# Gate products by Strassen's algorithm in a float32 graph network kernel

## The chip, the cores and the metric

One core of a Trainium2 chip. The metric is the device time of one execution in microseconds; medians of several runs are quoted. The engines are TensorE (PE; its weight loads are shown as PEld), VectorE (DVE), ScalarE (ACT), GpSimd (POOL) and the DMA queues. TensorE writes its products to PSUM, which these programs divide into eight banks; another engine then copies them to SBUF, the memory that holds all other tiles, and this copy is called an eviction. The granted clock is the share of its full clock that TensorE was given. Executions of one kernel agree within some 0.3%.

## The reference, cut to what matters

Sixty-four graphs of 256 nodes with 256 features go through three steps of a gated graph network (a GRU cell on aggregated messages), a residual and a layer norm, then through one graph attention layer with another residual and norm. All is float32.

```python
def _gru_cell(inp, h, w_ih, w_hh, b_ih, b_hh):
    gi = inp @ w_ih.T + b_ih              # 256 -> 768
    gh = h @ w_hh.T + b_hh                # 256 -> 768
    i_r, i_z, i_n = jnp.split(gi, 3, axis=-1)
    h_r, h_z, h_n = jnp.split(gh, 3, axis=-1)
    r = jax.nn.sigmoid(i_r + h_r)
    z = jax.nn.sigmoid(i_z + h_z)
    n = jnp.tanh(i_n + r * h_n)
    return (1.0 - z) * n + z * h

for i in range(L):                        # L = 3
    m = jnp.einsum('bnd,de->bne', h, weight[i])
    aggr = jnp.einsum('bst,bsd->btd', A, m)
    h = _gru_cell(aggr, h, w_ih, w_hh, b_ih, b_hh)
# then residual + layer norm, graph attention, residual + layer norm
```

## The kernel before

Graphs go through in pairs. A tile of [feature, (graph, node)] has 2 x 512 columns on 128 partitions and is the moving operand of the gate products, so each product has 512 columns. `weight[i] @ w_ih.T` is formed once. Two pairs are under way, half a pair apart; each yields between its steps, and the steps alternate, so that TensorE works on one pair while the other engines finish a step of the other. A scheduler then fixes the order of instructions on each engine. What follows the last n product of a layer until the new state is there (tanh, subtraction, product, sum) is called the tail.

```python
ps_t = ctx.enter_context(tc.tile_pool(name="ps_t", bufs=4, space=PSUM))   # transposes, small products
ps_g = ctx.enter_context(tc.tile_pool(name="ps_g", bufs=4, space=PSUM))   # gate products

def gates(i, e, ag, hT, hT_new, name):            # e: half of the 256 outputs
    def product(o, parts):
        pt = ps_g.tile([P, GN], F32, tag="g", name=f"pg_{name}_{o}")
        todo = [(w, m, d) for w, m in parts for d in range(C)]
        for n, (w, m, d) in enumerate(todo):
            nc.tensor.matmul(pt, w[:, d, o * P:(o + 1) * P], m[:, d, :],
                             start=(n == 0), stop=(n == len(todo) - 1))
        return pt
    hid, inp = (whhT, hT), (wc[:, i], ag)
    hn = product(2 * C + e, [hid])
    r_p = product(e, [hid, inp])
    ...                                            # sigmoid, n = tanh((hn + b) * r + n_p + b)
    nc.gpsimd.tensor_sub(d, hT[:, e, :], n)
    nc.vector.tensor_mul(d, d, z)
    nc.vector.tensor_add(hT_new[:, e, :], d, n)

steps = 3 + 3 * L + 2
while started < NP or active:
    if started < NP and (not active or (len(active) == 1 and active[0][1] >= steps // 2)):
        active.append([pair(started), 0])
        started += 1
    for a in list(active):
        ...                                        # one step of each pair
```

## Time and profile before

| | before |
|---|---|
| time, median | 2844.3 us |
| TensorE busy | 2803.1 us, 99% |
| TensorE's waits, summed | 30 us |
| VectorE / ScalarE / GpSimd busy | 1185.5 / 776.6 / 358.0 us |
| granted TensorE clock | 0.996 |

The page's first lines give the busy time of each engine and its share of the span, and the number of instructions. In a line of groups, the part ahead of the first bar names source line, engine, operation and tiles; then come busy time and the mean of one instruction; then the time the engine stood idle just before them and what ended it.

### The profile page before, as it was taken

How to read it: one execution, taken by the hardware profiler on the slowest of the kernel's cores; microseconds unless marked ns; L12 is line 12 of the kernel's file. 1: busy time of each engine (PE TensorE's matmuls, PEld its weight loads, DVE VectorE, ACT ScalarE, POOL GpSimd, SP SyncE). 2: the span in 40 equal slices, each digit the busy share in tenths (PEclk: the TensorE clock that was granted, in tenths of full speed). 3: DMA queues.
4: the chain of work that ended last, by engine and by line, in shares of the span. 5: the costliest groups of instructions: out<-in, count | busy, mean ns of one | idle time of the engine just before them, and what ended most of it. 6: DMA issues, size and time to landing. Idle time of an engine off the chain costs nothing.

```text
span 2842.6 us, 23364 instructions
## 1 busy us (share of the span) xinstructions
PE 2803.1 (99%) x8928; PEld 1560.3 (55%) x8928; DVE 1185.5 (42%) x2387; ACT 776.6 (27%) x1357; POOL 358.0 (13%) x362
## 2 busy tenths in 40 slices
PE   7999999999999999999999999999999999999996
PEld 4555555555555555555555555555555555555554
DVE  2344444444443444434443444443444444434434
ACT  1223222222322223222323222222222222222231
POOL 1111111111111111111111111111111111111111
PEclk9999999999999999999999999999999999999998
DMA  3000000000000000000000000000000000000000
GB/s 89 8 15 23 15 23 15 15 23 22 15 16 22 15 22 15 23 15 17 21 23 15 23 15 15 23 19 19 15 23 15 23 15 23 15 15 15 8 0 15
DMA packets 53518, 54.44 MB, mean 19 GB/s; under 512 B 1696, under 2 KB 53408, under 8 KB 53408
## 3 DMA queue, kind: packets, MB, share of 16 engines
q1 hardware_dynamic: 52256, 51.91, 5.6%
q8 instruction: 70, 1.15, 0.2%
q10 hardware_dynamic: 1056, 1.05, 0.1%
q14 instruction: 40, 0.33, 0.0%
q0 software_dynamic: 96, 0.01, 0.0%
HBM read 36.18 MB, written 16.78 MB: 19 GB/s over the span
## 4 chain that ended last, share of the span: by engine, by line
PE 98%; DVE 1%; DMA 0%; ACT 0%; issue 0%; POOL 0%; SPq 0%; POOLq 0%; DVEq 0%; ACTq 0%
PE pg L191 69%; PE pa L181 12%; PE pwh L270 4%; PE po L303 4%; PE pt L171 3%; PE s L263 2%; PE pt L162 2%; PE pt L294 1%; PE pw L138 1%; DMA adj<-in_adj_dram 0%; DVE d L210 0%; ACT z L207 0%; DVE hT L211 0%; PE pw L126 0%; DVE v L307 0%
## 5 line engine op out<-in xcount | busy, mean ns | idle before, releaser
L191 PE MATMUL pg<-ag,wc 128*128 128x512 f32 x2304 | 1051.4, 592 | 0.0
L191 PEld LDWEIGHTS pg<-ag,wc 128*128 128x128 f32 x2304 | 437.8, 190 | 551.0 <-issue 551.0
L191 PE MATMUL pg<-hT,whhT 128*128 128x512 f32 x1536 | 712.0, 592 | 0.0
L191 PEld LDWEIGHTS pg<-hT,whhT 128*128 128x128 f32 x1536 | 281.9, 190 | 278.8 <-issue 275.0
L202 DVE SCALAR_TENSOR_TENSOR n<-pg,bh,r 128x512 f32<-128x512 f32 x192 | 143.9, 750 | 603.8 <-ACT r L199 603.8
L199 ACT ACTIVATE r<-pg,b_sum 128x512 f32<-128x512 f32 x192 | 131.9, 687 | 859.8 <-PE pg L191 859.4
L191 PE MATMUL pg<-xT,whhT 128*128 128x512 f32 x768 | 350.5, 592 | 0.0
L210 DVE TENSOR_TENSOR d<-d,z 128x512 f32<-128x512 f32 x192 | 132.6, 691 | 522.0 <-ACT z L207 450.0
L209 POOL TENSOR_TENSOR d<-hT,n 128x512 f32<-128x512 f32 x128 | 162.1, 1267 | 1041.4 <-ACT n L204 1041.4
L181 PE MATMUL pa<-A,h 128*128 128x256 f32 x1024 | 239.3, 382 | 0.0
L204 ACT ACTIVATE n<-n,bi 128x512 f32<-128x512 f32 x192 | 138.5, 722 | 349.2 <-DVE n L203 349.2
L191 PEld LDWEIGHTS pg<-xT,whhT 128*128 128x128 f32 x768 | 143.5, 190 | 155.2 <-issue 146.1
L207 ACT ACTIVATE z<-pg,b_sum 128x512 f32<-128x512 f32 x192 | 132.1, 688 | 322.0 <-PE pg L191 322.0
L181 PEld LDWEIGHTS pa<-A,h 128*128 128x128 f32 x1024 | 191.9, 190 | 51.1 <-DVE h L72 12.1
L209 POOL TENSOR_TENSOR d<-xT,n 128x512 f32<-128x512 f32 x64 | 81.0, 1266 | 563.0 <-ACT n L204 563.0
L203 DVE TENSOR_TENSOR n<-n,pg 128x512 f32<-128x512 f32 x192 | 132.2, 689 | 32.5 <-PE pg L191 26.0
L211 DVE TENSOR_TENSOR hT<-d,n 128x512 f32<-128x512 f32 x192 | 131.9, 687 | 3.4
L171 PEld LDWEIGHTS pt<-ident,hT 128*128 128x128 f32 x768 | 88.4, 141 | 52.6 <-DVE hT L211 31.6
L270 PE MATMUL pwh<-gw,yT 128*128 128x257 f32 x512 | 116.7, 380 | 0.0
L303 PE MATMUL po<-wh,eT 128*128 128x256 f32 x512 | 116.5, 381 | 0.0
L181 PE MATMUL pa<-A,x 128*128 128x256 f32 x512 | 115.7, 379 | 0.0
L270 PEld LDWEIGHTS pwh<-gw,yT 128*128 128x128 f32 x512 | 97.5, 190 | 28.3 <-issue 8.5
(84 smaller groups left out, 1860.4 us busy)
## 6 DMA issues: line engine op xcount, KB each, us to landing
x<-in_x_dram SPq DMA_DIRECT2D x32, 512.0 KB, 3.8
adj<-in_adj_dram SPq DMA_DIRECT2D x32, 512.0 KB, 3.9
out_dram<-o SPq DMA_DIRECT2D x32, 512.0 KB, 2.9
wi_n<-in_L_gnn_w_ih_dram SPq DMA_DIRECT2D x1, 768.0 KB, 6.6
w_n<-in_L_gnn_weight_dram ACTq DMA_DIRECT2D x1, 768.0 KB, 9.4
wh_n<-in_L_gnn_w_hh_dram SPq DMA_DIRECT2D x1, 768.0 KB, 11.1
gw<-in_L_gnn_W_dram ACTq DMA_DIRECT2D x1, 256.0 KB, 10.4
bi<-in_L_gnn_b_ih_dram POOLq DMA_DIRECT2D x1, 3.0 KB, 8.1
```

The lines of the kernel that those rows point to most:

```text
L171: nc.tensor.transpose(pt[:, (c * C + d) * P:(c * C + d + 1) * P], hT[:, d, (g * C + c) * P:(g * C + c + 1) * P], ident)
L181: nc.tensor.matmul(pt[:, g * N:(g + 1) * N], h[:, g, s, d * P:(d + 1) * P], A[:, g, s, :], start=(s == 0), stop=(s == C - 1))
L191: nc.tensor.matmul(pt, w[:, d, o * P:(o + 1) * P], m[:, d, :], start=(n == 0), stop=(n == len(todo) - 1))
L199: nc.scalar.activation(r, r_p, AF.Sigmoid, bias=b_sum[:, e:e + 1])
L202: nc.vector.scalar_tensor_tensor(n, hn, bh[:, 2 * C + e:2 * C + e + 1], r, op0=ALU.add, op1=ALU.mult)
L203: nc.vector.tensor_add(n, n, n_p)
L204: nc.scalar.activation(n, n, AF.Tanh, bias=bi[:, 2 * C + e:2 * C + e + 1])
L207: nc.scalar.activation(z, z_p, AF.Sigmoid, bias=b_sum[:, C + e:C + e + 1])
L209: nc.gpsimd.tensor_sub(d, hT[:, e, :], n)
L210: nc.vector.tensor_mul(d, d, z)
L270: nc.tensor.matmul(pt[:, :D + 1], yT[:, d, k * P:(k + 1) * P], gw[:, d, :], start=(d == 0), stop=(d == C - 1))
L303: nc.tensor.matmul(pt[:, c * D:(c + 1) * D], eT[:, g, j, c * P:(c + 1) * P], wh[:, g, j, :], start=(j == 0), stop=(j == C - 1))
```

## The change

The gate matrix for r and z is 512 x 256, for n 256 x 256, and the moving tile is 256 x 512. Each is cut in 2 x 2 blocks, and seven block products of 256 columns take the place of eight (Strassen's algorithm in the form with shared sums). The weights' block sums are formed once. The moving tile's four block sums are formed on GpSimd for the state (`hT`) and for the aggregate (`ag`), and the products are put together by five VectorE sums of 512 for r and z and five for n. The products share three PSUM banks for r/z and three for n, so two banks are left for all else. To fit in SBUF, several tiles lose their second buffer. The diff is cut to what matters, and its lines are drawn together in places.

```diff
-    ps_t = ... bufs=4     ps_g = ... bufs=4
+    ps_t = ... bufs=2     ps_g = ... bufs=6
+    def blocks(m, name):
+        t = work.tile([P, 4, N], F32, tag="t", name=f"t_{name}", bufs=4)
+        b11, b12, b21, b22 = m[:, 0, :N], m[:, 0, N:], m[:, 1, :N], m[:, 1, N:]
+        nc.gpsimd.tensor_sub(t[:, 0:2, :], m[:, :, N:], m[:, 0, :].rearrange("p (g n) -> p g n", g=G))
+        nc.gpsimd.tensor_add(t[:, 2, :], t[:, 1, :], b11)
+        nc.gpsimd.tensor_sub(t[:, 3, :], b21, t[:, 2, :])
+        return {1: b11, 2: b21, 3: b22, 4: t[:, 3, :], 5: t[:, 0, :], 6: t[:, 2, :], 7: t[:, 1, :]}
+    class Products:                       # three banks x[0..2]; s, u2, u3 in SBUF
+        def product(self, q):
+            bank, fresh = {1: (0, True), 2: (0, False), 6: (1, True), 7: (1, False), 4: (1, False),
+                           5: (2, True), 3: (2, False)}[q]
+            ...                           # 256-column matmuls into self.x[bank]
+            if q == 1:   self.load(self.s, x1)
+            elif q == 6: nc.vector.tensor_add(self.u2, self.s, x2)
+            elif q == 7: nc.vector.tensor_add(self.u3, self.s, x2); nc.vector.tensor_add(self.u3, self.u3, x3)
+            elif q == 3: nc.vector.tensor_add(self.u2, self.u2, x3)
+            elif q == 4: nc.vector.tensor_add(self.s, self.s, x2)
+    # in gates(), first half:
+        for q in (1, 6, 5):
+            rz.product(q)
+        nn.product(1)
+        rz.product(7); update(1, rz.c[3])
+        nn.product(6)
+        rz.product(2); reset(0, rz.c[0], b_sum)
+        nn.product(5)
+        yield
+    # second half:
+        rz.product(3); reset(1, rz.c[1], b_rz)
+        nn.product(7)
+        rz.product(4); update(0, rz.c[2])
+        nn.product(2); fresh(0, 0, nn.c[0]); fresh(1, 1, nn.c[3])
+        nn.product(3); fresh(0, 1, nn.c[1]); finish(0)
+        nn.product(4); fresh(1, 0, nn.c[2]); finish(1)
```

`reset`, `update` and `fresh` form r, z and the argument of n's tanh, in pieces of one graph. `finish` is the old tail: tanh on ScalarE, `h - n` on GpSimd, product and sum on VectorE.

More of the change, by code (lines that the diff above doesn't have):

```diff
@@ L57 @@
     io = ctx.enter_context(tc.tile_pool(name="io", bufs=3))
-    work = ctx.enter_context(tc.tile_pool(name="work", bufs=2))
-    ps_t = ctx.enter_context(tc.tile_pool(name="ps_t", bufs=4, space=bass.MemoryType.PSUM))
-    ps_g = ctx.enter_context(tc.tile_pool(name="ps_g", bufs=4, space=bass.MemoryType.PSUM))
+    ps_t = ctx.enter_context(tc.tile_pool(name="ps_t", bufs=2, space=bass.MemoryType.PSUM))
+    ps_g = ctx.enter_context(tc.tile_pool(name="ps_g", bufs=6, space=bass.MemoryType.PSUM))
     def bank(name):
@@ L87 @@
     nc.gpsimd.memset(half, -0.5)
-    wihT = const.tile([P, C, O], F32, name="wihT")
     whhT = const.tile([P, C, O], F32, name="whhT")
@@ L93 @@
     wa2 = const.tile([P, C, P], F32, name="wa2")
+    w_sums = const.tile([P, L + 1, 4, 3 * P], F32, name="w_sums")
     b_sum = const.tile([P, O // P], F32, name="b_sum")
+    b_rz = const.tile([P, C], F32, name="b_rz")
     bi = const.tile([P, O // P], F32, name="bi")
@@ L99 @@
     with tc.tile_pool(name="prep", bufs=1) as prep:
+        wihT = prep.tile([P, C, O], F32, name="wihT")
         wi_n = prep.tile([P, O // P, D], F32, name="wi_n")
@@ L111 @@
         nc.vector.tensor_add(b_sum, bi, bh)
+        nc.vector.tensor_sub(b_rz, b_sum[:, :C], b_sum[:, C:2 * C])
         for src, dst in ((wi_n, wihT), (wh_n, whhT)):
@@ L140 @@
                     evacuate(wc[:, i, d, o0:o1], pt[:, :o1 - o0])
+        for j, w in enumerate([whhT] + [wc[:, i] for i in range(L)]):
+            for (a0, a1), (b0, b1), (o0, o1) in (((0, D), (D, 2 * D), (0, D)),
+                                                 ((2 * D, 2 * D + P), (2 * D + P, O), (D, D + P))):
+                a11, a12, a21, a22 = w[:, 0, a0:a1], w[:, 1, a0:a1], w[:, 0, b0:b1], w[:, 1, b0:b1]
+                s1, s2, s3, s4 = (w_sums[:, j, k, o0:o1] for k in range(4))
+                nc.gpsimd.tensor_add(s1, a21, a22)
+                nc.vector.tensor_sub(s3, a11, a21)
+                nc.gpsimd.tensor_sub(s2, s1, a11)
+                nc.gpsimd.tensor_sub(s4, a12, s2)
         gwT = transposed(gw, "gwT")
@@ L151 @@
             nc.vector.tensor_copy(wa2[:, d, :], wa[:, 1:2].to_broadcast([P, P]))
+    work = ctx.enter_context(tc.tile_pool(name="work", bufs=2))
     def to_T(src, name):
@@ L184, in aggregate @@
         return ag
-    def gates(i, e, ag, hT, hT_new, name):
-        def product(o, parts):
-            pt = ps_g.tile([P, GN], F32, tag="g", name=f"pg_{name}_{o}")
-            todo = [(w, m, d) for w, m in parts for d in range(C)]
-            for n, (w, m, d) in enumerate(todo):
-                nc.tensor.matmul(pt, w[:, d, o * P:(o + 1) * P], m[:, d, :],
-                                 start=(n == 0), stop=(n == len(todo) - 1))
-            return pt
-        hid, inp = (whhT, hT), (wc[:, i], ag)
-        hn = product(2 * C + e, [hid])
-        r_p = product(e, [hid, inp])
-        r = work.tile([P, GN], F32, tag="r", name=f"r_{name}")
-        nc.scalar.activation(r, r_p, AF.Sigmoid, bias=b_sum[:, e:e + 1])
-        n_p = product(2 * C + e, [inp])
-        n = work.tile([P, GN], F32, tag="n", name=f"n_{name}")
-        nc.vector.scalar_tensor_tensor(n, hn, bh[:, 2 * C + e:2 * C + e + 1], r, op0=ALU.add, op1=ALU.mult)
-        nc.vector.tensor_add(n, n, n_p)
-        nc.scalar.activation(n, n, AF.Tanh, bias=bi[:, 2 * C + e:2 * C + e + 1])
-        z_p = product(C + e, [hid, inp])
-        z = work.tile([P, GN], F32, tag="z", name=f"z_{name}")
-        nc.scalar.activation(z, z_p, AF.Sigmoid, bias=b_sum[:, C + e:C + e + 1])
-        d = work.tile([P, GN], F32, tag="d", name=f"d_{name}")
-        nc.gpsimd.tensor_sub(d, hT[:, e, :], n)
-        nc.vector.tensor_mul(d, d, z)
-        nc.vector.tensor_add(hT_new[:, e, :], d, n)
@@ new lines, in rows, with __init__ @@
+    def rows(j, first, second, o0):
+        w = whhT if j == 0 else wc[:, j - 1]
+        n = first[1] - first[0]
+        s = [w_sums[:, j, k, o0:o0 + n] for k in range(4)]
+        return {1: w[:, 0, first[0]:first[1]], 2: w[:, 1, first[0]:first[1]], 3: s[3],
+                4: w[:, 1, second[0]:second[1]], 5: s[0], 6: s[1], 7: s[2]}
+    class Products:
+        def __init__(self, terms, tag, name, load):
+            self.terms, self.load = terms, load
+            self.x = [ps_g.tile([P, 2 * N], F32, tag="g", name=f"x{k}_{name}") for k in range(3)]
+            self.s, self.u2, self.u3 = (work.tile([P, 2 * N], F32, tag=f"{tag}{k}", name=f"{tag}{k}_{name}")
+                                        for k in ("s", "u", "v"))
+            self.c = [self.x[0], self.u2, self.s, self.u3]
+        def product(self, q):
+            bank, fresh = {1: (0, True), 2: (0, False), 6: (1, True), 7: (1, False), 4: (1, False),
+                           5: (2, True), 3: (2, False)}[q]
+            for half, parts in enumerate(self.terms):
+                for n, (w, m, e) in enumerate(parts):
+                    nc.tensor.matmul(self.x[bank][:, half * N:(half + 1) * N], w[q][:, e * P:(e + 1) * P], m[q],
+                                     start=(fresh and half == 0 and n == 0), stop=(n == len(parts) - 1),
+                                     skip_group_check=True)
+            x1, x2, x3 = self.x
+            if q == 1:
+                self.load(self.s, x1)
+            elif q == 6:
+                nc.vector.tensor_add(self.u2, self.s, x2)
+            elif q == 7:
+                nc.vector.tensor_add(self.u3, self.s, x2)
+                nc.vector.tensor_add(self.u3, self.u3, x3)
+            elif q == 3:
+                nc.vector.tensor_add(self.u2, self.u2, x3)
+            elif q == 4:
+                nc.vector.tensor_add(self.s, self.s, x2)
@@ new lines, in gates, with both, with_bias, reset @@
+    def gates(i, ag, hT, hT_blocks, hT_new, name):
+        ag_blocks = blocks(ag, f"ag_{name}")
+        def both(first, second, o0):
+            return (rows(0, first, second, o0), hT_blocks), (rows(i + 1, first, second, o0), ag_blocks)
+        def with_bias(dst, src):
+            for e in range(C):
+                nc.scalar.activation(dst[:, e * N:(e + 1) * N], src[:, e * N:(e + 1) * N], AF.Identity,
+                                     bias=b_sum[:, C + e:C + e + 1])
+        hid, inp = both((0, D), (D, 2 * D), 0)
+        rz = Products([[(*hid, e), (*inp, e)] for e in range(C)], "rz", f"rz_{name}", with_bias)
+        hid_n, inp_n = both((2 * D, 2 * D + P), (2 * D + P, O), D)
+        nn = Products([[(*hid_n, 0)], [(*inp_n, 0)]], "nn", f"nn_{name}", nc.scalar.copy)
+        r = work.tile([P, C, G, N], F32, tag="r", name=f"r_{name}")
+        z = work.tile([P, C, G, N], F32, tag="z", name=f"z_{name}")
+        n = work.tile([P, C, G, N], F32, tag="n", name=f"n_{name}")
+        d = r
+        def reset(g, src, bias):
+            for e in range(C):
+                nc.scalar.activation(r[:, e, g, :], src[:, e * N:(e + 1) * N], AF.Sigmoid, bias=bias[:, e:e + 1])
+        def update(g, src):
+            nc.scalar.activation(z[:, :, g, :], src.rearrange("p (e n) -> p e n", e=C), AF.Sigmoid)
+        def fresh(e, g, src):
+            nc.vector.scalar_tensor_tensor(n[:, e, g, :], src[:, :N], bh[:, 2 * C + e:2 * C + e + 1], r[:, e, g, :],
+                                           op0=ALU.add, op1=ALU.mult)
+            nc.vector.tensor_add(n[:, e, g, :], n[:, e, g, :], src[:, N:])
+        def finish(e):
+            n_e, d_e = (v[:, e].rearrange("p g n -> p (g n)") for v in (n, d))
+            nc.scalar.activation(n_e, n_e, AF.Tanh, bias=bi[:, 2 * C + e:2 * C + e + 1])
+            nc.gpsimd.tensor_sub(d_e, hT[:, e, :], n_e)
+            nc.vector.tensor_mul(d_e, d_e, z[:, e].rearrange("p g n -> p (g n)"))
+            nc.vector.tensor_add(hT_new[:, e, :], d_e, n_e)
+        for q in (1, 6, 5):
+            rz.product(q)
+        nn.product(1)
+        rz.product(7)
+        update(1, rz.c[3])
+        nn.product(6)
+        rz.product(2)
+        reset(0, rz.c[0], b_sum)
+        nn.product(5)
+        yield
+        rz.product(3)
+        reset(1, rz.c[1], b_rz)
+        nn.product(7)
+        rz.product(4)
+        update(0, rz.c[2])
+        nn.product(2)
+        fresh(0, 0, nn.c[0])
+        fresh(1, 1, nn.c[3])
+        nn.product(3)
+        fresh(0, 1, nn.c[1])
+        finish(0)
+        nn.product(4)
+        fresh(1, 0, nn.c[2])
+        finish(1)
@@ L237, in pair @@
         hT = to_T(x_sb, f"xT_{p}")
+        hT_blocks = blocks(hT, f"xT_{p}")
         yield
         h = x_sb
-        v = work.tile([P, G, C, D], F32, tag="v", name=f"v_{p}")
+        v = work.tile([P, G, C, D], F32, tag="v", name=f"v_{p}", bufs=1)
         for i in range(L):
@@ L243, in pair @@
             hT_new = work.tile([P, C, GN], F32, tag="hT", name=f"hT_{p}_{i}", bufs=4)
-            for e in range(C):
-                gates(i, e, ag, hT, hT_new, f"{p}_{i}_{e}")
-                yield
+            yield from gates(i, ag, hT, hT_blocks, hT_new, f"{p}_{i}")
+            yield
             hT = hT_new
             if i < L - 1:
+                hT_blocks = blocks(hT, f"hT_{p}_{i}")
                 h = work.tile([P, G, C, D], F32, tag="h", name=f"h_{p}_{i}")
@@ L263, in pair @@
             nc.tensor.matmul(s2, wa2[:, d, :], yT[:, d, :], start=(d == 0), stop=(d == C - 1))
-        wh = work.tile([P, G, C, D], F32, tag="wh", name=f"wh_{p}")
+        wh = work.tile([P, G, C, D], F32, tag="wh", name=f"wh_{p}", bufs=1)
         s1 = work.tile([P, K], F32, tag="s1", name=f"s1_{p}")
-        sc = work.tile([P, K, N], F32, tag="sc", name=f"sc_{p}")
+        sc = work.tile([P, K, N], F32, tag="sc", name=f"sc_{p}", bufs=1)
         for k in range(K):
@@ L276, in pair @@
         nc.vector.scalar_tensor_tensor(sc, sc, ALPHA, sc, op0=ALU.mult, op1=ALU.max)
-        em = work.tile([P, K, N], F32, tag="em", name=f"em_{p}")
+        em = work.tile([P, K, N], F32, tag="em", name=f"em_{p}", bufs=1)
         nc.gpsimd.memset(em, NEG_INF)
@@ L287, in pair @@
         yield
-        eT = work.tile([P, G, C, N], F32, tag="eT", name=f"eT_{p}")
+        eT = work.tile([P, G, C, N], F32, tag="eT", name=f"eT_{p}", bufs=1)
         for g in range(G):
@@ L308, in pair @@
                                                y[:, g, c, :], op0=ALU.mult, op1=ALU.add)
-        o_sb = work.tile([P, G, C, D], F32, tag="o", name=f"o_{p}")
+        o_sb = work.tile([P, G, C, D], F32, tag="h", name=f"o_{p}")
         layer_norm(v, o_sb, f"b_{p}")
```

## The prediction

> **What bounds the kernel now.** First I read the page's busy shares, its slices and the shares by engine of the chain that ended last, because they say which engine sets the time.
>
> ```profile
> PE 2803.1 (99%) x8928; PEld 1560.3 (55%) x8928; DVE 1185.5 (42%) x2387; ACT 776.6 (27%) x1357; POOL 358.0 (13%) x362
> ...
> PE 98%; DVE 1%; DMA 0%; ACT 0%; issue 0%; POOL 0%; SPq 0%; POOLq 0%; DVEq 0%; ACTq 0%
> ```
>
> TensorE (PE) is busy from end to end and makes up 98% of the chain. Everything else is hidden beside it. Next the groups, for the price of each operation:
>
> ```profile
> L191 PE MATMUL pg<-ag,wc 128*128 128x512 f32 x2304 | 1051.4, 592 | 0.0
> L191 PE MATMUL pg<-hT,whhT 128*128 128x512 f32 x1536 | 712.0, 592 | 0.0
> ...
> L202 DVE SCALAR_TENSOR_TENSOR n<-pg,bh,r 128x512 f32<-128x512 f32 x192 | 143.9, 750 | 603.8 <-ACT r L199 603.8
> ...
> L210 DVE TENSOR_TENSOR d<-d,z 128x512 f32<-128x512 f32 x192 | 132.6, 691 | 522.0 <-ACT z L207 450.0
> L209 POOL TENSOR_TENSOR d<-hT,n 128x512 f32<-128x512 f32 x128 | 162.1, 1267 | 1041.4 <-ACT n L204 1041.4
> ```
>
> The mean of one matmul (592 ns) contains overlap, so the rate is read from the timeline, where products follow each other without a gap:
>
> ```profile
> 1408.44 3.60 PE L191 MATMUL pg<-hT,whhT 128*128 128x512 f32 x8
> 1418.74 3.62 PE L181 MATMUL pa<-A,x 128*128 128x256 f32 x16
> 1418.74 3.21 PEld L181 LDWEIGHTS pa<-A,x 128*128 128x128 f32 x15 [0.24 <-issue]
> ```
>
> Eight of 512 columns start in 3.43 us (the next group starts at 1411.88), 0.43 us each; sixteen of 256 columns take the same, 0.215 us each. So 256 columns cost exactly half, although a weight load (0.19 us) then nearly fills its slot. A product in the program is two such instructions, so one 256-column product is 0.43 us. Groups of 24 gate instructions recur in the chain at 109.87 and 196.43 us: a pair of graphs takes 86.56 us, 32 pairs 2770, and 73 us are start and end.
>
> Last, the very end, where one pair runs alone and PE has to wait:
>
> ```profile
> 2810.82 1.94 PE L162 MATMUL pt<-ident,y 128*128 128x128 f32 x8 [4.62 <-DVE y L225]
> 2813.22 3.78 PE L263 MATMUL s<-yT,wa 128*128 128x512 f32 x4 [0.46 <-ACT yT L70]
> 2827.29 2.38 PE L294 MATMUL pt<-ident,sc 128*128 128x128 f32 x8 [6.57 <-ACT sc L284]
> ```
>
> The eight transposes take 1.04 us elsewhere and four 512-column instructions some 1.9. After gaps of 4.6 and 6.6 us they take twice that; the granted clock of the last 92 us is 0.88. A long PE gap costs more than itself.
>
> **What the Trainium skill says.** "TensorE: Matmul & The Clock Gate", Part 1, says that after an idle window of about 3.4 us the array runs at half clock until it has been busy for such a window. The three lines above agree. The same page, in its architectural detail, says that VectorE and ScalarE are strict first-in-first-out. The trace agrees in that every idle time there ends in one wait, and it means that an instruction waiting on GpSimd holds up all behind it. "GPSIMD Engine Reference", section 3.1, gives 4497 ns for a two-input add of 2048 elements. The trace has 1267 ns for 512; the line through both gives about 0.73 us for 256 (an estimate). "SBUF — State Buffer", Who interferes with whom, says that a VectorE instruction with two SBUF inputs and a GpSimd instruction that reads SBUF block each other for a whole instruction. In the stretch of the trace I looked at they never overlap, so no number is to be had before.
>
> **The change part by part.** Removed: the gates are 24 products of 512 columns per layer and pair, 24 x 0.86 = 20.6 us. Now they are 28 + 14 = 42 of 256, 42 x 0.43 = 18.1 us. Saved 2.5 us, times 96 layer-pairs = 247 us. With nothing else, 2844 becomes about 2600.
>
> Added on GpSimd: two sets of block sums per layer and pair, each 1.27 + 0.73 + 0.73 = 2.7 us, so 5.5 x 96 = 524 us more; 880 in all, no bound as a sum. Added on VectorE: ten sums of 512 (0.69 each) and the n gate in eight pieces of 256 (about 0.42 to 0.45) for four of 512; 6.9 + 3.4 + 2.8 = 13.1 us instead of 5.6. That is +7.5 x 96 = 720 us, 1900 in all, some 60 us of VectorE per pair, against about 79 us of PE. No engine becomes a bound by its sum. The question is latency.
>
> I therefore took the compiled order of the changed kernel on each engine for one pair in the steady state and laid these durations along it by hand, with 0.05 to 0.1 us per hand-over, 0.26 us from the last matmul to its reader, and about 0.60 us between independent VectorE sums of 512 (as before's timeline shows). PE work is 79.4 us per pair. The places where PE's next instruction isn't ready:
>
> 1. Layer 0, second half, **7.9 us**. PE has 16 gate products and 8 transposes, 7.9 us. VectorE has in that stretch the other pair's residual add and layer norm (until 5.3 us, with a wait for GpSimd's power in it), then twelve gate sums and n pieces up to 11.4. Then the tail: tanh 0.72, GpSimd subtraction 2 x 1.27, product and sum. The new state is there at about 15.8 us, and PE's next instruction transposes it.
> 2. Layer 1, first half, **3.2 us**. With two transpose banks for four, one of them held by the score row until the last score is read, each attention projection waits for the eviction of the one before (about 1.2). Then the aggregate's second half is evicted behind 3.7 us of masking on VectorE and needs 2.0 us of GpSimd before product 6 (1.7).
> 3. End of layer 1 into layer 2, **7.3 us**. The state is at 13.8, while PE is through with gates and attention output at 10.3 (3.5); the block sums of the state, 2.0 us on GpSimd, stand before the next hidden products (1.7); eviction behind the second layer norm (0.7); aggregate block sums (1.4).
> 4. Layer 2 into the next pair's layer 0, **1.7 us** for the aggregate's block sums. The state's transposes are hidden behind 11 us of gate products.
>
> Sum 20.1: a period of 79.4 + 20.1 = 99.5 us, times 32 = 3184. Start and end: 73 as before, about 10 for forming the weight sums on GpSimd, and I allow 30 more because a pair alone has nothing to fill these waits: **3297 us**. So the 8 us saved per pair come back as 20 us of waits.
>
> **The rivals.** (a) The waits are filled and the saving arrives: 2600 to 2750. For it: in before PE has almost no waits in the middle, and the changed order moves hidden products ahead of the aggregate as filler. Against it: that filler is already in my timetable, and in layer 0 nothing is left between the last gate product and the state. (b) Some of the waits are shorter than I lay them, saving and waits cancel, 2790 to 2900. This needs 12 of the 20 us to be wrong. (c) The waits have consequences. GpSimd's second subtraction blocks VectorE's product of two SBUF tiles (0.6 us at the end of layers 0 and 1, about 1.2 at the aggregate after layer 2: 2.4 per pair). The half clock after gap 1 costs about 2.5 us, as the last lines above show (1.9 + 3.8 us for what takes about 3), and sometimes 1 us after gap 3. Together up to 6 us per pair, 190 us: about 3480. (d) Weight loads become the bound at 256 columns: the 3.62 us line speaks against it.
>
> **Range and chances.** The timetable says 3297, (c) pulls up by as much as 190. My errors of a hand timetable (the same wait counted at two places, a reorder that hides one) and the author's evident care over the order of products pull down. I take **3280 us**, with 3040 to 3470 for 8 in 10: 12 to 25 us of waits and after-effects per pair. Slower by over 2%: 0.88; within 2%: 0.05; faster: 0.07.
>
> **What would show it.** PE's own work: gate matmuls of 256 columns, 8064 instructions, at 0.215 us, so PE busy near 2550 to 2650 in the longer span (about 80%). VectorE busy near 1900, GpSimd near 880. In the waits, the largest of PE should be the transposes waiting for the new state (VectorE's last sum), about 11 us per pair, then gate products waiting for GpSimd's block sums, about 5 to 6. The granted clock should be below 1 in the middle slices, which (c) needs. GpSimd or VectorE two-input instructions with longer durations than 1267 and 690 ns would show the port. I am wrong if PE stays above 95% busy, if VectorE's sums are shorter than 0.69 us, or if transposes of the state wait less than 3 us a pair.

## The result and the profile after

The changed kernel takes **3569.4 us**, against 2844.3: 1.255 times as long. It was predicted to be slower, 3280 us with a range of 3040 to 3470, so the direction came out, the waits nearly did, and the price of the half clock behind them did not: the measured time lies above the range.

The page of the changed kernel: busy shares, the granted clock in 40 slices, and the chain that ended last by engine.

```profile
PE 2864.1 (80%) x12384; PEld 2352.9 (66%) x12384; DVE 1962.8 (55%) x3740; ACT 906.9 (25%) x1837; POOL 938.1 (26%) x962
...
PEclk9999898989998998989999889989899898989898
...
PE 54%; DVE 26%; POOL 13%; issue 4%; ACT 3%; DMA 0%; POOLq 0%; DVEq 0%; ACTq 0%; SPq 0%
```

TensorE is busy for 80% of a longer span, and its busy time has grown by 61 us although it has an eighth less gate arithmetic. The clock is down in most slices (0.906 in the mean). The chain now runs through VectorE and GpSimd for 39% of the span.

The view of waits of the changed kernel, TensorE's own, with the total in us, the number and the longest:

```profile
PE pt L192 <- DVE hT L293: 357.8, 65, 7.3
PE x_rz L239 <- POOL t_ag L212: 215.7, 96, 3.9
PE x_rz L239 <- POOL t_hT L212: 38.5, 31, 1.5
PE x_nn L239 <- DVE nnv_nn L248: 25.0, 31, 0.8
PE pa L202 <- DVE wh L78: 20.9, 31, 0.7
```

All of TensorE's waits sum to 692 us, and 692 + 2864 = 3556 of the span of 3565. So there are two items to explain: waits of 662 us more than before, and 61 us more busy time where 247 less was expected.

The timeline of the changed kernel, TensorE in the stretch at the end of layer 0 and into layer 1 (start, duration, what, and idle time with its releaser):

```profile
1691.79 0.60 PE L183 MATMUL pt<-ident,y 128*128 128x128 f32 x4
1699.71 0.45 PE L192 MATMUL pt<-ident,hT 128*128 128x128 f32 x1 [7.33 <-DVE hT L293]
1699.95 1.06 PE L239 MATMUL x_rz<-hT,whhT 128*128 128x256 f32 x2
1700.81 1.70 PE L192 MATMUL pt<-ident,hT 128*128 128x128 f32 x7
1702.33 2.75 PE L371 MATMUL s<-yT,wa 128*128 128x512 f32 x4
```

A gap of 7.33 us, then half speed for some 4 us: a product of two 256-column instructions takes 1.06 us (0.59 elsewhere in the same view), and four of 512 columns, which reach into full speed again, 2.75 us. What VectorE did meanwhile, in the same stretch:

```profile
1694.36 0.42 DVE L286 TENSOR_TENSOR n<-n,nns_nn 128x256 f32<-128x256 f32 x1
1696.63 2.33 DVE L292 TENSOR_TENSOR r<-r,z 128x512 f32<-128x512 f32 x2 [1.86 <-POOL r L291]
1698.89 1.28 DVE L293 TENSOR_TENSOR hT<-r,n 128x512 f32<-128x512 f32 x2
```

VectorE ends the n pieces at 1694.78, 2.4 us after TensorE ran dry; then comes the tail through ScalarE and GpSimd, and the first of the two products (line 292) waits inside for GpSimd: the group of line 292 has a mean of 1379 ns where before's line 210 had 691 (in the changed kernel the median is 1733 and the least 677).

The other long gap, at the aggregate of layer 0, in TensorE's timeline:

```profile
1666.38 1.03 PE L239 MATMUL x_rz<-t_xT,w_sums 128*128 128x256 f32 x4
1671.02 1.22 PE L239 MATMUL x_rz<-t_ag,w_sums 128*128 128x256 f32 x2 [3.62 <-POOL t_ag L212]
1672.03 1.06 PE L239 MATMUL x_rz<-t_xT,w_sums 128*128 128x256 f32 x2
1672.88 1.91 PE L239 MATMUL x_rz<-t_ag,w_sums 128*128 128x256 f32 x4
```

VectorE and GpSimd ahead of it, from the same timeline:

```profile
1665.77 1.74 DVE L292 TENSOR_TENSOR r<-r,z 128x512 f32<-128x512 f32 x1 [2.23 <-POOL r L291]
1667.43 0.68 DVE L78 COPY ag<-pa 128x512 f32<-128x512 f32 x1
1668.19 1.64 POOL L211 TENSOR_TENSOR t_ag<-ag 128x512 f32<-128x512 f32 x1 [1.23 <-DVE ag L78]
1669.91 1.05 POOL L212 TENSOR_TENSOR t_ag<-t_ag,ag 128x256 f32<-128x256 f32 x1
```

The aggregate's products were through by 1664.81, but its eviction (line 78) stands behind the other pair's held-up product and comes at 1667.43; then the block sums take 1.64 and 1.05 us instead of 1.27 and 0.73.

How much the half clock costs can be read from the granted clock. These windows lie on the three stretches of half clock of one pair, behind the gap into layer 2 (3.54 us and soon 1.23 more), the gap of 3.62 and the gap of 7.33. After the length come the busy times of PE, PEld, VectorE, ScalarE and GpSimd with their instructions, then the clock:

```profile
1632.23:1639.06 6.83, 5.60 (x18) 4.22 (x17) 4.13 (x15) 0.59 (x1) 3.95 (x5) 0.50 0.01 2
1669.78:1676.60 6.82, 5.58 (x13) 4.51 (x14) 2.32 (x3) 0.00 (x0) 2.16 (x3) 0.50 0.00 0
1697.08:1703.91 6.83, 4.20 (x12) 2.97 (x13) 4.39 (x6) 0.59 (x1) 3.46 (x4) 0.50 0.01 2
```

Half of TensorE's busy time in them is lost: 2.8, 2.8 and 2.1 us, 7.7 us a pair. The clock record of the whole run has 97 such stretches; TensorE is busy for 492 us in them, so 246 us are lost. That is most of the 308 us (61 + 247) by which busy time is too long.

### The profile page after: what moved, and what is told of

Same layout as the page of the kernel before. It is cut to its first block, busy times and chain, and to the rows that moved or that the text cites. A ratio compares the mean times of both kernels' runs of the same rounds, so it can differ in the third digit from the quotient of the medians.

```text
span 3565.2 us, 32872 instructions
## 1 busy us (share of the span) xinstructions
PE 2864.1 (80%) x12384; PEld 2352.9 (66%) x12384; DVE 1962.8 (55%) x3740; ACT 906.9 (25%) x1837; POOL 938.1 (26%) x962
## 3 DMA queue, kind: packets, MB, share of 16 engines
q10 hardware_dynamic: 1056, 1.05, 0.1%
## 4 chain that ended last, share of the span: by engine, by line
PE 54%; DVE 26%; POOL 13%; issue 4%; ACT 3%; DMA 0%; POOLq 0%; DVEq 0%; ACTq 0%; SPq 0%
PE x_rz L239 27%; PE x_nn L239 10%; PE pa L202 5%; DVE r L292 5%; POOL t_ag L211 4%; PE pwh L378 4%; POOL r L291 3%; PE pt L192 3%; DVE n L284 3%; PE s L371 2%; POOL t_ag L212 2%; DVE n L286 2%; ACT n L290 2%; DVE ag L78 2%; DVE hT L293 1%
## 5 line engine op out<-in xcount | busy, mean ns | idle before, releaser
L239 PE MATMUL x_rz<-t_ag,w_sums 128*128 128x256 f32 x1152 | 393.6, 442 | 215.7 <-POOL t_ag L212 215.7
L192 PE MATMUL pt<-ident,hT 128*128 128x128 f32 x768 | 174.2, 370 | 357.8 <-DVE hT L293 357.8
L239 PEld LDWEIGHTS x_rz<-t_ag,w_sums 128*128 128x128 f32 x1152 | 243.4, 219 | 290.7 <-POOL t_ag L212 254.3
L291 POOL TENSOR_TENSOR r<-hT,n 128x512 f32<-128x512 f32 x128 | 159.7, 1270 | 724.1 <-ACT n L290 724.1
L292 DVE TENSOR_TENSOR r<-r,z 128x512 f32<-128x512 f32 x192 | 259.8, 1379 | 153.5 <-POOL r L291 153.5
L239 PE MATMUL x_rz<-t_hT,w_sums 128*128 128x256 f32 x768 | 257.2, 426 | 38.5 <-POOL t_hT L212 38.5
L202 PE MATMUL pa<-A,h 128*128 128x256 f32 x1024 | 242.3, 385 | 20.9 <-DVE wh L78 20.9
L239 PE MATMUL x_rz<-ag,wc 128*128 128x256 f32 x768 | 228.4, 379 | 0.0
L239 PEld LDWEIGHTS x_rz<-t_hT,w_sums 128*128 128x128 f32 x768 | 154.8, 211 | 67.7 <-POOL t_hT L212 50.9
L239 PE MATMUL x_rz<-hT,whhT 128*128 128x256 f32 x512 | 173.4, 423 | 0.0
L239 PE MATMUL x_nn<-t_ag,w_sums 128*128 128x256 f32 x576 | 171.3, 379 | 0.0
## 6 DMA issues: line engine op xcount, KB each, us to landing
wh_n<-in_L_gnn_w_hh_dram SPq DMA_DIRECT2D x1, 768.0 KB, 11.2
```

Source lines behind the costliest of these rows:

```text
L192: nc.tensor.transpose(pt[:, (c * C + d) * P:(c * C + d + 1) * P], hT[:, d, (g * C + c) * P:(g * C + c + 1) * P], ident)
L202: nc.tensor.matmul(pt[:, g * N:(g + 1) * N], h[:, g, s, d * P:(d + 1) * P], A[:, g, s, :], start=(s == 0), stop=(s == C - 1))
L239: nc.tensor.matmul(self.x[bank][:, half * N:(half + 1) * N], w[q][:, e * P:(e + 1) * P], m[q], start=(fresh and half == 0 and n == 0), sto ...
L291: nc.gpsimd.tensor_sub(d_e, hT[:, e, :], n_e)
L292: nc.vector.tensor_mul(d_e, d_e, z[:, e].rearrange("p g n -> p (g n)"))
```

## The experiments

Times are medians. "Waits" is the sum of TensorE's waits in the profile, "busy" its busy time; together they make up the span within 0.7%. Kernels named b_ start from the kernel before, e_ from the changed one; all e_ kernels give right results.

| run | us | ratio to before | waits | busy | clock |
|---|---|---|---|---|---|
| before | 2844 | 1 | 30 | 2803 | 0.996 |
| changed | 3569 | 1.255 | 692 | 2864 | 0.906 |
| b_21 (wrong result) | 2618 | 0.921 | 53 | 2556 | 0.995 |
| b_256 | 2852 | 1.003 | 31 | 2810 | 0.996 |
| b_ps26 | 2941 | 1.034 | 96 | 2831 | 0.996 |
| e_warm | 3521 | 1.238 | 430 | 3081 | 0.971 |
| e_warm2 | 3423 | 1.204 | 369 | 3043 | 0.988 |
| e_dvefin | 3354 | 1.179 | 572 | 2774 | 0.931 |
| e_order | 3355 | 1.180 | 597 | 2748 | 0.945 |
| e_stag4 | 3559 | 1.252 | 691 | 2859 | 0.898 |
| e_all | 3229 | 1.135 | 476 | 2742 | 0.931 |
| e_three0 | 3299 | 1.160 | 483 | 2804 | 0.947 |
| e_three | 2971 | 1.045 | 263 | 2692 | 0.978 |
| e_three2 | 2969 | 1.044 | 271 | 2687 | 0.976 |
| e_three5 | 2940 | 1.034 | 277 | 2648 | 0.989 |
| e_three3 | 2892 | 1.017 | 211 | 2666 | 0.980 |
| e_three4 | 2920 | 1.027 | 217 | 2693 | 0.975 |
| e_three6 | 2824 | 0.993 | 174 | 2632 | 0.991 |
| e_three7 | 2915 | 1.026 | 236 | 2670 | 0.985 |

### Is the saving real? b_21 and b_256

b_21 leaves 3 of the 24 products out of the kernel before and adds nothing, so it has Strassen's arithmetic without its price.

```diff
             todo = [(w, m, d) for w, m in parts for d in range(C)]
+            if o >= 2 * C and parts[0][1] is hT or o == 2 * C - 1:
+                todo = todo[:-1]
```

> The kernel before with 3 of the 24 gate products per layer and pair left out, so TensorE's arithmetic is that of Strassen and nothing is added; the result is wrong on purpose. Theory A (the saving in arithmetic is real, 2.58 us per layer and pair): 2590 to 2615 us with TensorE still above 97% busy. Theory B (the other engines could not keep up even then): above 2680.

2618.5 us, 3.5 above theory A's range, with TensorE 98% busy. Busy time fell by 246.8 us, the predicted 247 almost to the digit. The time fell by 225: TensorE, now faster, waits 26 us for the new state in 34 places. So even the kernel before had only about a tail's worth of work beside its tail.

b_256 issues each product as two of 256 columns.

```diff
-            for n, (w, m, d) in enumerate(todo):
-                nc.tensor.matmul(pt, w[...], m[:, d, :], ...)
+            for g in range(G):
+                for n, (w, m, d) in enumerate(todo):
+                    nc.tensor.matmul(pt[:, g * N:(g + 1) * N], w[...], m[:, d, g * N:(g + 1) * N], ...)
```

> The kernel before with every gate product issued as two of 256 columns, without Strassen. Theory A (256 columns cost half of 512, 0.215 us an instruction, weight loads still hidden): 2844 within 1%. Theory B (weight loads of 0.19 us become the bound at 256 columns and eat part of the saving): 2900 to 3050.

2852 us, 0.3% more, as theory A has it. The page's first line of that run shows how near the weight loads come:

```profile
PE 2810.3 (99%) x13536; PEld 2429.3 (85%) x13536; DVE 1185.4 (42%) x2387; ACT 776.6 (27%) x1357; POOL 357.8 (13%) x362
```

With 85% of the span in weight loads they are still hidden. The rate of 256-column products isn't where the time went.

### What do the banks cost? b_ps26

```diff
-    ps_t = ... bufs=4     ps_g = ... bufs=4
+    ps_t = ... bufs=2     ps_g = ... bufs=6
```

> The kernel before with the changed kernel's split of the PSUM banks alone (two for transposes and small products, six for gates). The prediction laid 1.2 us per pair on the two banks: 2844 plus 20 to 60 us. If the banks are hidden beside gate products here: 2844 within 0.5%.

2941 us, 97 more than before: a miss on both sides. In the kernel before, the split costs 3.0 us a pair and not the 1.2 laid in the prediction; the waits for the two banks come to 64 us there, with gate products only between the first two attention projections. In the changed kernel such products stand between more of them, and these waits come to 29 us in all (20.9 and 8.2).

### The clock: e_warm and e_warm2

Both put 13 dummy products of 512 columns per pair (with the identity as weights, into a bank that nobody reads any more) where TensorE waits. e_warm's dummies read z:

```diff
         fresh(1, 0, nn.c[2])
         finish(1)
+        if i < L - 1:
+            keep_busy(rz.x[0], z[:, 1].rearrange("p g n -> p (g n)"), (7, 3)[i])
...
-        for q in (1, 6, 5):
+        rz.product(1)
+        if i == 0:
+            keep_busy(nn.x[2], ag[:, 1, :], 3)
+        for q in (6, 5):
             rz.product(q)
```

> The changed kernel with 13 dummy products of 512 columns per pair of graphs put into the three longest gaps of TensorE (7 and 3 after the last gate product of layers 0 and 1, 3 ahead of product 6 in layer 0); the result stays right. Theory A (beyond the waits, the time is lost because matmuls after a gap of 3.5 us or more run at half clock, some 9.5 us per pair): the granted clock rises from 0.906 to above 0.97, the waits for the new state fall since dummies stand in them, and the time falls by 150 to 300 us, to 3270 to 3420, although TensorE does 11 us more work per pair. Theory B (the excess over the prediction is waits that I laid too short, or the port): the time stays within 2% of 3569 or rises.

3521 us: by the letter theory B's result, although the clock rose to 0.971. The accounts show why it is no answer. Thirteen dummies are 26 instructions of 0.43 us, 358 us in 32 pairs; the waits shrank by 262 only, so 96 us of dummies stood ahead of other work (three of them before the attention output, some before an n product), and 141 us of busy time beyond the dummies was saved. The test was badly placed. e_warm2 makes the dummies read values that come up inside the gaps:

```diff
+        if i == 0:
+            keep_busy(rz.x[0], nn.u2, 7)
+        elif i == 1:
+            keep_busy(rz.x[0], n[:, 0].rearrange("p g n -> p (g n)"), 3)
```

> As the run with dummies before, which raised the clock to 0.971 and gained only 48 us, but the dummies now wait for values that come up inside the gaps, so they stand in the gaps and not ahead of other work: 7 after the other pair's transposes in layer 0, 3 within the attention output in layer 1, 3 ahead of product 6 in layer 0. Theory A (half clock costs some 7.5 us per pair: 2.2 after the gap of layer 0, 2.7 after that of layer 1, 2.7 after the aggregate's): the matmul stretches after the three gaps run at 0.215 us an instruction again and the time falls by 130 to 240 us, to 3330 to 3440. Theory B (work at half clock was only hidden wait; what follows waits for GpSimd and VectorE anyway): the time stays above 3490 although the clock is full.

3423 us, 146 less than the changed kernel and inside theory A's range, with 358 us more work on TensorE. Now the waits fell by 323, nearly what the dummies take, and busy time without the dummies is 3043 - 358 = 2685, 179 less than 2864. The gain is clock alone: counted as above, the half clock costs 31 us in this run instead of 246. The same stretch of the timeline as above, in e_warm2:

```profile
1626.43 6.25 PE L257 MATMUL x_rz<-nnu_nn,ident 128*128 128x512 f32 x14 [0.47 <-DVE nnu_nn L251]
1633.30 0.30 PE L192 MATMUL pt<-ident,hT 128*128 128x128 f32 x1 [0.62 <-DVE hT L297]
1633.82 1.26 PE L192 MATMUL pt<-ident,hT 128*128 128x128 f32 x7 [0.21 <-DVE hT L297]
1634.91 0.60 PE L239 MATMUL x_rz<-hT,whhT 128*128 128x256 f32 x2
1635.34 1.88 PE L382 MATMUL s<-yT,wa 128*128 128x512 f32 x4
```

The state arrives no earlier after the last n product than it did, but the four instructions of 512 columns take 1.88 us and not 2.75, and the gate product 0.60 and not 1.06.

### One latency at a time: e_dvefin and e_order

e_dvefin moves one subtraction.

```diff
-            nc.gpsimd.tensor_sub(d_e, hT[:, e, :], n_e)
+            nc.vector.tensor_sub(d_e, hT[:, e, :], n_e)
```

> One part undone: the subtraction h - n at the end of a layer goes from GpSimd to VectorE. Theory A (the tail of a layer is a latency chain, two GpSimd subtractions of 1.27 us and a VectorE product that is held up by the second one, 1379 ns in the mean for 691): the product falls to about 690 ns, the wait of the state's transposes falls from 358 us to 200 to 270, the aggregate's wait after layer 2 shrinks too, and some gaps become too short to cost clock; 3250 to 3420 us. Theory B (VectorE is the bound in the second half of a layer, so that another 0.6 us per piece on it costs what GpSimd's latency did): 3520 or more.

3354 us, 215 less, with VectorE 32 us busier. Waits fell by 120 us (the state's from 358 to 287, the aggregate's from 216 to 154) and busy time by 90. The group of the products that follow, changed kernel first, then e_dvefin:

```profile
L292 DVE TENSOR_TENSOR r<-r,z 128x512 f32<-128x512 f32 x192 | 259.8, 1379 | 153.5 <-POOL r L291 153.5
```

```profile
L292 DVE TENSOR_TENSOR r<-r,z 128x512 f32<-128x512 f32 x192 | 142.3, 770 | 0.0
```

With the GpSimd subtraction gone from beside it, the product takes 770 ns in the mean (its median is 686). The time is in theory A's range; the state's wait, laid at 200 to 270 us, fell less. The run removes GpSimd's latency and the hold on VectorE's product together and does not divide its gain between them. The stretches of half clock fell from 97 to 68, the loss in them from 246 to 150 us: the gap of 3.6 us at layer 0's aggregate shrank to 1.7.

e_order issues the three products that need no block sums of the aggregate first.

```diff
-        for q in (1, 6, 5):
-            rz.product(q)
-        nn.product(1)
-        rz.product(7); update(1, rz.c[3])
-        nn.product(6)
-        rz.product(2); reset(0, rz.c[0], b_sum)
+        rz.product(1)
+        nn.product(1)
+        rz.product(2); reset(0, rz.c[0], b_sum)
+        for q in (6, 5):
+            rz.product(q)
+        nn.product(6)
+        rz.product(7); update(1, rz.c[3])
         nn.product(5)
```

> The changed kernel with the three products that need no block sums of the aggregate issued first (rz 1, n 1, rz 2, then 6, 5). Theory A (product 6 waits for a chain eviction, 1.27 to 1.6 us and 0.73 us on GpSimd, with only 1.7 to 2.6 us of products ahead of it): TensorE's wait for the aggregate's block sums falls from 216 us to under 70, the long gap in layer 0 and the half clock behind it go, 3290 to 3420 us. Theory B (the wait only moves, to product 2 that waits for the copy of product 1, or to the state's transposes): 3500 or more.

3355 us, 214 less. The time is as theory A has it, the wait isn't quite: it fell from 216 to 139 us, because the scheduler still put a product that needs the sums (6) ahead of product 2 in layers 1 and 2, where 1.6 us remain. The gap of 3.6 us in layer 0 shrank to 1.3, and with it went the half clock behind it: busy time fell by 116 us, more than the waits did (96). Counted as above, the half clock costs 113 us in this run.

### What lies beside the tail: e_stag4, e_all, e_three0, e_three

e_stag4 starts the second pair four steps behind the first instead of seven.

```diff
-(len(active) == 1 and active[0][1] >= steps // 2)
+(len(active) == 1 and active[0][1] >= 4)
```

> The changed kernel with the second pair started four steps behind the first and not seven, so that a layer's first half of one pair (11 us of products) stands between the last gate product of the other and its state's transposes. Theory A (the waits for the state are a matter of what lies beside the tail): the wait of the state's transposes falls from 358 us to under 150, the granted clock rises to 0.94 or more, 3120 to 3350 us. Theory B (VectorE, 62 us per pair with bursts, is what limits; another order only moves the waits): above 3450.

3559 us, 0.3% less: theory B by the number. TensorE's waits in that run:

```profile
PE x_rz L239 <- POOL t_ag L212: 250.2, 96, 3.6
PE pt L192 <- DVE hT L293: 238.0, 64, 7.3
PE pt L183 <- DVE y L332: 126.9, 16, 7.9
```

The state's waits fell by 120 us, as meant. But a first half of the other pair that follows a tail at once has its aggregate's eviction queued behind that tail on VectorE, so more aggregate gaps are of 3.6 us (250 instead of 216 us), and a new wait came, the second pair's layer norm with nothing beside it (127 us). The waits moved.

e_all takes the stagger of four, e_order's order and e_dvefin's subtraction together.

> Stagger of four, the order with 1, 1, 2 first, and the subtraction on VectorE together. If the waits are separate latencies they add up: about 215 less 150 to 250 each, 2850 to 3080 us with TensorE over 90% busy. If VectorE (about 2030 us busy) becomes the bound in the gate stages, 3100 or more. To beat the kernel before it would have to keep less than 7 us of waits per pair.

3229 us, by the number the second theory's (3100 or more), though VectorE is busy for only 64% of the span. The three together save 340 us, the two single gains without the stagger 429. For some 80 us of each two pairs TensorE runs without a wait. What stays are ends of layers (in each two pairs 6.1 us at one end of layer 1, 2.6 at one of layer 0 and 2.6 at one of layer 2, 188 us in all), the layer norm (137) and the aggregate's block sums (75).

So the stagger has to be such that both tails have work. With three pairs under way, five steps apart and the youngest first in each round, a first half of another pair (26 products, 11 us) stands between the last gate product and the state's transposes in every layer.

```diff
-        if started < NP and (not active or (len(active) == 1 and active[0][1] >= steps // 2)):
+        if started < NP and (not active or active[-1][1] >= 5):
...
-        for a in list(active):
+        for a in reversed(list(active)):
```

A fifth buffer for the state and a third for the mask are paid for by letting the attention weights share a tile. e_three0 is this alone; e_three has e_order's order and e_dvefin's subtraction too.

> Three pairs under way alone, with the changed kernel's own order of products and its subtraction on GpSimd. Theory A: the state's waits go (below 60 us from 358), the aggregate's block sums stay as the wait (216 us or more), 2850 to 3080 us. Theory B: above 3250, as with the stagger of four, where the waits only moved.

> Three pairs under way, started five steps apart, the youngest first in each round, with the order 1, 1, 2 and the subtraction on VectorE (one more buffer for the state and the mask, one less for the attention weights). In this order a layer's first half of another pair, 11 us of products, stands between the last gate product and the state's transposes in every layer, and other work stands beside the second layer norm. Theory A (what eats Strassen's saving is tails without work beside them, and clock behind those gaps; no engine is a bound by its sum): TensorE over 94% busy, clock above 0.97, 2680 to 2830 us, so faster than the kernel before. Theory B (VectorE, 64 us per pair with waits for GpSimd and ScalarE in strict order, is the bound in practice): 2900 to 3150.

e_three0: 3299 us, theory B's range by the number (above 3250). The waits are as theory A says: the state's are gone (18 us), the aggregate's stay (247). But VectorE is late in a stretch where a layer norm, evictions and gate sums meet (172 us of waits there), and the half clock stays, behind the aggregate's gaps and behind gaps of only 2.3 to 2.5 us in that stretch: it costs 159 us. e_three: 2971 us, 599 less than the changed kernel, and inside theory B's range, above theory A's. So tails without work beside them were not all; VectorE's order limits too, though it is busy for only 71% of the span. The state's waits are 15 us. What is left are VectorE's late sum (73 us), evictions of yT (61) and the aggregate's block sums (76).

### The rest: e_three2 to e_three7

e_three2 computes the score row after the four attention projections, so that it doesn't hold a bank. e_three5 adds the scaling of the layer norms on ScalarE; e_three3 instead evicts transposes into the feature layout and the aggregates by ScalarE alone; e_three4 has both.

```diff
-            evacuate(dst[:, d, :], pt)          # ScalarE and VectorE in turn
+            nc.scalar.copy(dst[:, d, :], pt)
...
-            evacuate(ag[:, d, :], pt)
+            nc.scalar.copy(ag[:, d, :], pt)
```

> Three pairs as before, with the score row computed after the four attention projections, so that it no longer holds one of the two small banks while they run. If the bank's hold matters: TensorE's waits in the projections and the aggregate behind them shrink, 10 to 50 us less than 2971. If these waits are VectorE's backlog: within 10 us of 2971.

> As e_three2, with the scaling of both layer norms on ScalarE (eight pieces of some 0.45 us per pair) and off VectorE, where it waits for GpSimd's power in strict order. If VectorE's backlog in that stage is the cause: the n product's wait for its sum (73 us) falls below 20 and the waits for yT shrink, 2830 to 2920 us. If not: above 2940.

> As e_three2, with transposes into the feature layout and aggregates evicted by ScalarE alone (0.59 us a piece instead of 0.69 on VectorE, five pieces a pair). Backlog theory: VectorE busy falls by some 110 us and the waits for evictions with it, 2850 to 2940. If ScalarE's own order (it waits for VectorE's sums to form r and z) holds evictions up: 2960 or more.

> Both: layer norm scaling and the evictions on ScalarE. Backlog theory: 2760 to 2860 us, TensorE above 95% busy, and perhaps below the kernel before (2844). If ScalarE becomes the late one: no better than the better of the two alone.

2969, 2940, 2892 and 2920 us. The bank's hold costs nothing by now (2 us). Taking work off VectorE gains 29 or 77 us: e_three3 is inside its backlog range; e_three5 falls between its two, the n sum's wait gone but the waits for yT up from 60 to 93 us. Both together are worse than the evictions alone: the n sum's wait is gone, but 68 us of waits for yT, evicted by ScalarE, and 25 for the scaled rows have come. All waits sum to only 6 us more than in e_three3; busy time is 27 us more, for behind the gap of 2.3 us before the aggregate sixteen instructions take 5.29 us where 3.6 is usual. One queue's lateness was exchanged for another's, in a place where the clock is lost.

e_three6 shortens the chain to product 6, which needs two of the four block sums; the big instruction had formed an unneeded one with the first of them.

```diff
-        nc.gpsimd.tensor_sub(t[:, 0:2, :], m[:, :, N:], m[:, 0, :].rearrange("p (g n) -> p g n", g=G))
+        nc.gpsimd.tensor_sub(t[:, 1, :], b22, b12)
         nc.gpsimd.tensor_add(t[:, 2, :], t[:, 1, :], b11)
+        nc.gpsimd.tensor_sub(t[:, 0, :], b12, b11)
```

> As e_three3, with the first block subtraction split in two, so that product 6 waits for two GpSimd pieces of 0.73 us and not for 1.27 and 0.73. If the wait is this chain: the aggregate's waits fall from 81 us to 20 to 45, 2830 to 2870 us. If it is the eviction ahead of it: within 10 us of 2892.

2823.6 us: 68 less than e_three3 and 6 below the expected range, with the aggregate's waits down from 81 to 33 us. That is just below the kernel before (0.993, interval 0.992 to 0.995), and 21% below the changed kernel. Its page and TensorE's longest waits:

```profile
PE 2631.7 (93%) x12384; PEld 2197.1 (78%) x12384; DVE 1884.2 (67%) x3772; ACT 991.4 (35%) x1997; POOL 749.6 (27%) x962
```

```profile
PE x_nn L240 <- DVE nnv_nn L249: 51.9, 31, 1.7
PE x_rz L240 <- POOL t_ag L212: 33.4, 30, 1.1
PE pa L202 <- ACT yT L184: 28.5, 28, 1.2
```

The same 12384 matmul instructions as in the changed kernel take 232 us less busy time at a clock of 0.991. Counted as above, the half clock costs 13 us here and 246 there, a difference of 233.

e_three7 puts rz product 4 behind n products 2 and 3, to give VectorE time before n product 4.

> As e_three6, with rz product 4 issued after the n products 2 and 3, to give VectorE 1.7 us more before n product 4 overwrites what it reads. If this wait (62 us) is only lateness of VectorE: 30 to 60 us less than e_three6, 2780 to 2840, level with or below the kernel before. If VectorE's backlog just moves it: within 15 us of e_three6.

2915 us, 92 worse. The wait it was meant for stayed at 51.9 us, and the aggregate's block sums are waited for 119 us again: with another order of issue the scheduler laid the filling products elsewhere. The expectation missed; why the scheduler chose so was not followed up.

## Why the prediction was wrong, point by point

**What bounds before, and the saving: right.** b_21 saves 247 us of TensorE's work, and 256 columns take half the time of 512 (b_256).

**No engine becomes a bound by its sum: right.** VectorE came to 1963 us (1900 predicted) and GpSimd to 938 (880), in a span of 3565; and e_three6 runs below before with VectorE still at 1884.

**The waits laid along the compiled order: right in sum, in part by luck.** Predicted 20.1 us a pair; the gaps of one pair in the timeline sum to 20.7. By place: layer 0, 7.9 against 8.1 (7.33 and 0.80); layer 1, 3.2 against 2.6; into layer 2, 7.3 against 6.4 (3.54, 1.23, 1.58); into the next pair, 1.7 against 3.6. Only the last is off by much. There the eviction stands behind the product that GpSimd's subtraction holds up, which rival (c) had put at 1.2 us more, and the block sums are slower beside VectorE. At the ends of the layers the product is held up too (1733 ns), the timetable had not counted it, and other terms there were too long by about as much. By kind, the state's transposes wait 11.2 us a pair (about 11 predicted), products for block sums 7.9 (5 to 6). Two smaller points: PE work was put at 79.4 us a pair, while the prediction's own numbers give 86.56 - 3 x 2.58 = 78.8. And that every idle time of the profile ends in one wait is how the profile names a releaser, no evidence of an engine's order; the eviction that stands behind the held-up product is.

**The step that failed** is the size of the consequences in rival (c), "The half clock after gap 1 costs about 2.5 us, as the last lines above show (1.9 + 3.8 us for what takes about 3), and sometimes 1 us after gap 3." The runs showed half clock behind three gaps of every pair, costing 2.1 us after gap 1, 2.8 after gap 3 and 2.8 after gap 4: 7.7 us a pair and 246 us in all, where (c) had at most 3.5 a pair and the middle of the forecast none. The first was right. I had read the price of a gap from two gaps of before and applied it to one; gap 3 was laid at its true 3.5 us and got "sometimes 1", and gap 4 was laid at 1.7 us, measured 3.62, and got nothing. The experiments confirm the cause and the size: e_warm2 filled the gaps and recovered 146 us of time and 179 of busy time; e_three6, with the same instructions, has 232 us less busy time and 233 less by the count of half clock. Against b_21, with the same gate arithmetic, e_three6 is busy for 76 us more; 8 of these are half clock by the same count (13 against 6), 7 are what halving the instructions costs in b_256, and the rest was not taken apart.

**The second error was the choice of the middle.** The timetable gave 3297 without any after-effect and (c) put up to 190 us on top. I took 3280 for errors of a hand timetable and "the author's evident care over the order of products", which no view supported. The start and end were laid at 113 us; 32 periods of 109.23 us (aggregate of layer 1 at 1602.76 and 1711.99) leave 70, an error of 43 that helped. So the account is 32 x (79.4 work + 20.7 waits) + 70 = 3273, the half clock adds 246, and 46 us of the span of 3565 stay unaccounted for.

**The rivals.** (a) and (b) fell. (d) fell with b_256. (c) was the right one, and too small.

**Shown and only argued.** Shown: the waits and where they are; that filling gaps brings the clock and time back; that taking the tail's subtraction off GpSimd, or issuing products that need no block sums first, is each worth some 215 us with its clock; that the waits move when the stagger changes, and that work beside the tails removes them. Only argued or open: what the rest of the 76 us is, how e_dvefin's gain divides between GpSimd's latency and the hold on VectorE, and why the scheduler moved the filling products in e_three7.

## What to carry to other kernels

An operation that the bounding engine is spared is worth its time only if the work put in its place has something to run beside: lay the compiled order of every engine along the measured durations, find where the bounding engine's next instruction isn't ready, and count the clock lost after each such gap, not only the gap. If it doesn't pay, look first at the distance between the units under way and at the length of the chain to the first dependent instruction: here three pairs instead of two, another order of products, a shorter chain and a less crowded VectorE turned 1.255 into 0.993 with the same arithmetic. Even then an eighth fewer gate products (225 us, as b_21 has it) left 20 us, so a cut in arithmetic should be weighed against what its extra passes cost the other engines.

## What the Trainium skill lacked or had wrong

- "TensorE: Matmul & The Clock Gate", HAM oscillation: it names gaps of more than about 3.4 us as the ones to avoid. Here shorter ones were enough, and not every time. Two gaps of e_three0, the eight instructions behind the first at full clock and behind the second at half:

```profile
1607.72 1.99 PE L202 MATMUL pa<-A,x 128*128 128x256 f32 x8 [2.45 <-DVE yT L78]
1708.21 3.68 PE L202 MATMUL pa<-A,x 128*128 128x256 f32 x8 [2.46 <-DVE yT L78]
```

By the clock record, half clock followed 29 of 30 gaps of 2.0 to 2.4 us in e_three4, and 15 of 60 gaps of 1.5 to 2.0 in e_three7. The page's next section has frequent short idle times as a second cause, without their lengths. What such a gap costs it works out for a kernel of its own; here it was 2.1 to 2.8 us.

- "SBUF — State Buffer", Who interferes with whom: the runs agree for VectorE, whose product of two SBUF tiles took up to 1.75 us for 0.69 beside a GpSimd subtraction of 1.27. GpSimd loses too: its subtraction for the aggregate took 1.64 us beside VectorE's sum and product above, and 1.58 in the median of the run instead of 1.27. The page has factors for such pairs, but no durations by shape.
- "GPSIMD Engine Reference", section 3.1: nothing wrong; the estimate of 0.73 us for 256 elements, drawn from its figure and one of the trace, was measured at 0.72 to 0.73, and at 1.05 beside VectorE's product.
